# Local attention in a six-stage kernel: values for shifted keys computed, or put together by transfers

## The chip, the cores and the metric

The kernel runs on one core of one Trainium2 chip, as one program with one launch. The time is device time in microseconds (us), the median of three runs. The engines are PE (TensorE; PEld are its weight loads), DVE (VectorE), ACT (ScalarE), POOL (GpSimd) and SP (SyncE, which issues most transfers). All data are 32-bit floats except masks and a few small operands in bf16.

## The reference

Eight sequences of 256 tokens, 128 channels, pass through four layers of different kinds: a gated linear recurrence followed by local attention with a feed-forward block (twice), a Mamba block with a mixture of experts, multi-head attention with a feed-forward block and a second mixture of experts, and a last attention with a ternary linear layer. Only the local attention matters here; it has 8 heads of 64 channels and a window of 64:

```python
bk, bv = (look_around(bk), look_around(bv))   # keys of the window before and of the own window
sim = jnp.einsum('bhwid,bhwjd->bhwij', bq, bk)
mask = (i < j) | (i > j + WINDOW) | (j == -1)
sim = jnp.where(mask, -jnp.finfo(sim.dtype).max, sim)
attn = jax.nn.softmax(sim, axis=-1)
out = jnp.einsum('bhwij,bhwjd->bhwid', attn, bv)
```

So each window of 64 queries sees 128 keys: its own window and the one before. Of a sequence of 256 tokens, window 0 and 1 need keys 0 to 127, window 2 needs keys 64 to 191, window 3 keys 128 to 255. The order of the keys within such a set doesn't matter to the result, as long as scores, mask and values have the same order.

## The kernel before

**Stages.** The program has six stages: `rglru` (the recurrence), `local_mamba` (local attention with its feed-forward block, twice, then Mamba, for each sequence), `moe1`, `chunked` (multi-head attention), `moe2`, `typed` (the last layer). In the profile `local_mamba` runs from about 46 us to 790 us; `chunked` begins at about 860, `moe2` at 1270, `typed` at 1440.

**`local_mamba`.** `one_sequence` runs two local blocks (`local_block`, l = 0 and 1) for a sequence; `mamba_sequence` then takes its result. `interleave` keeps four sequences of local blocks in flight, beside the second half of the recurrence and the Mamba of the sequences before. There are 8 x 2 = 16 local blocks.

**A local block.** `local_qk` makes four products of 128 tokens x 512 channels (q and k, two token tiles each; tile `qk`), with norms and rotation on ACT, DVE and POOL, and transposes q and k to channels x tokens. `local_attention` then makes the values: three products `vps`, for tokens 0 to 127, 64 to 191 and 128 to 255, each copied by ACT (L1128) to slot 0, 1 or 2 of tile `v`. Both `qk` and `vps` take their PSUM from tag Q, which has two buffers in this stage. Then, for each of two query tiles: a mask product and the score products into `sc`, the maximum on DVE (`nm`, L1147), eight Exps on ACT (`e`, L1153), a reciprocal on DVE (`rc`, L1157), a scaling on POOL (L1158), eight transposes (`pt`, L981) with copies to `ptsb`, and the output products `o`, which read `v` as the operand that is held. `parts` tells which queries use which keys and which slot:

```python
parts = (((0, P, 0, 0),), ((128, 64, 64, 1), (192, 64, 128, 2)))   # first query, queries, first key, slot of v
```

The first query tile (queries 0 to 127) uses slot 0; of the second, queries 128 to 191 use slot 1 (keys 64 to 191) and queries 192 to 255 use slot 2. The bf16 mask `band` has one column block of 128 keys for each query tile.

**Mamba.** For each sequence, `mamba_sequence` has eight steps m = 0 to 7. A step needs two transfers on SP (`bc`, L1269, 256 KB each, three buffers), four Exps on ACT (`da`, L1302, three buffers), on DVE the product `hs<-u,bc` (L1304), the scan (L1306) and the product `hs<-hs,bc` (L1307), and on PE two products `y`. The `bc` come from a small table `xs` in DRAM that SP writes first (L1261). A `bc` buffer is free once L1307 of three steps earlier is done.

**What sets the order.** The Python code only records the instructions. `_Order` then plans the order on each engine: a list scheduler that takes, among the instructions that are ready, the one of lowest rank, with durations from `LENGTHS`, per-name shifts of rank from `BIAS` (keyed by engine, tile and stage), and `STAY`, a penalty for leaving a PE tile shape or an ACT function table. The planned order is imposed as the program's order on each engine, so every engine, and SP's queue too, works through a fixed list.

Of the kernel before, what the change touches and what calls it, by code (L numbers as in the profile page):

```python
# [23 lines left out]
P = 128  # L24
# [57 lines left out]
def _tables():  # L82
    f = np.float32
    cols, n = [], 0
# [9 lines left out]
    half = np.arange(0, 64, 2, dtype=f)  # L94
# [47 lines left out]
    def mask(bad):  # L142
        return np.where(bad, f(NEG), f(0))
# [3 lines left out]
    w = i % 64  # L147
    madd("band", np.concatenate([mask((i < k0) | (i > k0 + 64)), mask((k0 < w) | (k0 > w + 64))], 1))
# [163 lines left out]
class _Order:  # L312
# [14 lines left out]
    STAY = dict(PE=80, ACT=740)  # L327
    BIAS = {
        "ACT  1": 100, "ACT  5": 585, "ACT bt 3": 5, "ACT bt 5": -775, "ACT d 2": -425, "ACT da 2": -45, "ACT e 2": -5, "ACT e 4": 965, "ACT e 6": -20,
        "ACT got 3": 575, "ACT h 2": -200, "ACT ix 4": 15, "ACT k 2": 265, "ACT lavp 2": 210, "ACT lnrs 1": -10, "ACT lnrs 2": -160, "ACT lnsq 1": -135,  # L330
        "ACT lnsq 2": 15, "ACT ot 2": 10, "ACT ptsb 2": -595, "ACT ptsb 6": -515, "ACT q 2": 20, "ACT qsq 2": 10, "ACT r 2": -5, "ACT rg 1": 10,
        "ACT rg 2": -915, "ACT rn 2": 15, "ACT rs 4": 340, "ACT rs 6": -690, "ACT s 6": 200, "ACT sakq 2": -10, "ACT sg 3": -550, "ACT sh 5": -2525,
        "ACT spe 1": -220, "ACT spt 1": -50, "ACT st 6": 100, "ACT sz 2": 280, "ACT v 2": 885, "ACT vs 4": 320, "ACT xchunked 2": 15, "ACT xs 2": -610,
        "DVE biasfull 3": -335, "DVE biaspart 3": -20, "DVE bt 5": -5, "DVE c 1": 590, "DVE centre 0": 320, "DVE d 2": 10, "DVE decaypart 4": -600,
        "DVE e 4": 570, "DVE four 4": 100, "DVE fs 4": -70, "DVE gate 4": 340, "DVE get 2": 200, "DVE got 4": 530, "DVE identb 0": -50, "DVE k 6": 500,
        "DVE lg 2": 2240, "DVE lo 4": -265, "DVE mv 4": -660, "DVE mv 5": 100, "DVE mv 6": -485, "DVE nm 2": -3975, "DVE nm 6": 4960, "DVE nth 4": -45,
        "DVE oh 2": -725, "DVE oh 5": -10, "DVE ptsb 2": -3895, "DVE ptsb 6": 895, "DVE put 4": -395, "DVE put 5": 55, "DVE q 5": -825, "DVE q 6": -475,
        "DVE rc 2": -1225, "DVE rc 6": 10, "DVE route 2": -55, "DVE s 5": 10, "DVE sares 2": 70, "DVE sel 2": -1590, "DVE sg 3": -140, "DVE sm 4": 2720,
        "DVE spl 1": -215, "DVE ss 2": 370, "DVE st 4": 85, "DVE st 6": 1645, "DVE sum 4": 170, "DVE t 2": 440, "DVE u 2": 250, "DVE vs 4": 50,
        "DVE we 4": 1425, "DVE xc 2": 460, "DVE xla 4": -15, "DVE xlocal 2": -5, "DVE xmoe 5": -200, "DVE xmoe 6": -580, "DVE xpf 4": -370,  # L340
        "DVE xrglru 2": 120, "DVE xsa 4": 80, "DVE z 4": -1990, "PE a 2": -100, "PE acc 5": 155, "PE b 2": -35, "PE bt 3": 75, "PE bt 5": 50,
        "PE cum 2": -995, "PE cum 4": -25, "PE cum 5": -615, "PE fold 2": 2915, "PE g 2": -4155, "PE gate 2": 785, "PE kps 4": 135, "PE less 2": 295,
        "PE lg 2": 1680, "PE lg 4": 50, "PE ln 2": -10, "PE o 2": 10, "PE o 6": -10, "PE pg 5": 150, "PE ps 4": -15, "PE pt 4": -130, "PE pu 3": 220,
        "PE py 3": -200, "PE py 5": 170, "PE qk 2": 25, "PE qkt 2": -720, "PE raw 2": -8675, "PE rows 2": 400, "PE sc 2": -50, "PE sc 4": 65, "PE sc 6": 5,
        "PE v 5": 290, "PE vps 2": 4075, "PE vps 4": 25, "PE wo 2": 75, "PE wo 6": -85, "PE wout 2": -115, "PE xin 2": 1180, "PE xps 2": -2540, "PE y 2": 20,
        "PE z 2": -450, "PE zt 5": 560, "PE zt 6": 25, "POOL d 2": 130, "POOL e 6": -30, "POOL got 4": -200, "POOL h 2": 370, "POOL k 5": 400,
        "POOL k 6": 850, "POOL km 6": 1240, "POOL mean 0": 1510, "POOL places 5": -200, "POOL q 6": 20, "POOL rest 4": -65, "POOL rg 1": -800,
        "POOL rg 2": -200, "POOL rot 2": -400, "POOL s 6": -750, "POOL t 2": 550, "POOL zero 0": -655, "POOL zeros 1": 385, "SP bc 2": -970, "SP cst 3": 5,
        "SP got 3": 355, "SP got 5": 350, "SP rottable 0": 80, "SP rows 4": 210, "SP rowschunked 4": -105, "SP vec 0": -830, "SP w 0": 15, "SP w 3": 115,
        "SP wattn 2": 585, "SP wffn 2": 705, "SP wlocal 0": 1175, "SP wmoe 4": 520, "SP xs 2": -105, "SP ybuf 5": -200,  # L350
    }
    LENGTHS = {
        "ACT  LoadActFuncSet  ": (1178, 1283), "ACT d Ln 128x512 128x512": (535, 640), "ACT da Exp 128x255 128x255": (398, 503),
        "ACT e Abs 128x256 128x256": (460, 565), "ACT e Exp 128x128 128x128": (420, 525), "ACT e Exp 128x256 128x256": (461, 566),
        "ACT e Exp 128x512 128x512": (527, 632), "ACT four Exp 128x2 128x2": (100, 205), "ACT got DMACopy 128x512 128x512": (454, 3611),
        "ACT h TensorCopy 64x255 64x255": (295, 400), "ACT lnrs Exp 128x256 128x256": (315, 420), "ACT ot TensorCopy 128x512 128x512": (486, 591),
        "ACT qsq Square 128x512 128x512": (494, 599), "ACT r Relu 128x256 128x256": (460, 565), "ACT rg Exp 128x1020 128x1020": (1039, 1144),
        "ACT rg Exp 128x1024 128x1024": (998, 1103), "ACT rg Ln 128x1024 128x1024": (950, 1055), "ACT rn Exp 128x16 128x16": (110, 215),
        "ACT rn Ln 128x16 128x16": (112, 217), "ACT rs Exp 128x2 128x2": (96, 201), "ACT rs Ln 128x2 128x2": (98, 203),
        "ACT sh Silu 128x512 128x512": (492, 597), "ACT v TensorCopy 128x512 128x512": (485, 590), "ACT xc Identity 128x256 128x256": (460, 565),  # L360
        "ACT xc Silu 128x512 128x512": (526, 631), "ACT xchunked TensorCopy 128x256 128x256": (263, 368), "ACT xmoe Identity 128x256 128x256": (404, 509),
        "ACT xs TensorCopy 33x256 33x256": (257, 362), "ACT xsq Square 128x128 128x128": (297, 402), "DVE biaspart TensorCopy 96x256 96x256": (197, 282),
        "DVE decay TensorScalarPtr 128x512 128x512": (508, 593), "DVE decaypart TensorCopy 128x512 128x512": (331, 416),
        "DVE four TensorScalarPtr 128x4 128x4": (76, 160), "DVE ge TensorScalarPtr 128x256 128x256": (380, 465),
        "DVE ge TensorScalarPtr 85x256 85x256": (372, 457), "DVE got TensorScalarPtr 128x128 128x128": (258, 343),
        "DVE h TensorTensor 128x256 128x256": (312, 397), "DVE hs TensorScalarPtr 128x1024 128x1024": (2189, 2274),
        "DVE hs TensorTensor 128x1024 128x1024": (1116, 1201), "DVE mv BNStatsAggregate 128x2 128x6": (82, 167),
        "DVE nm TensorTensor 128x8 128x8": (66, 151), "DVE ptsb TensorCopy 128x512 128x512": (589, 674), "DVE rc Reciprocal 128x16 128x16": (160, 245),
        "DVE rc Reciprocal 128x4 128x4": (84, 169), "DVE rc Reciprocal 128x8 128x8": (106, 191), "DVE rg TensorScalarPtr 128x256 128x256": (577, 662),
        "DVE rg TensorTensor 128x1024 128x1024": (1109, 1194), "DVE rottable TensorScalarPtr 128x256 128x256": (261, 346),  # L370
        "DVE s TensorScalarPtr 128x128 128x128": (247, 332), "DVE s TensorTensor 128x256 128x256": (323, 408),
        "DVE sm TensorReduce 128x16 128x512": (593, 678), "DVE ss TensorReduce 128x8 128x512": (594, 679), "DVE st BNStats 128x6 128x128": (197, 282),
        "DVE sum TensorReduce 128x32 128x448": (810, 895), "DVE t TensorScalarPtr 128x256 128x256": (384, 469),
        "DVE t TensorTensor 128x512 128x512": (593, 678), "DVE vec TensorTensor 128x1 128x1": (59, 144), "DVE vec TensorTensor 85x1 85x1": (59, 144),
        "DVE vs TensorCopy 128x512 128x512": (594, 679), "DVE wlocal TensorScalarPtr 128x682 128x682": (481, 566),
        "DVE x TensorScalarPtr 128x256 128x256": (368, 453), "DVE xc TensorScalarPtr 128x254 128x254": (383, 468),
        "DVE xc TensorScalarPtr 128x255 128x255": (384, 469), "DVE xla TensorScalarPtr 128x256 128x256": (442, 527),
# [394 lines left out]
class _Kernel:  # L772
# [346 lines left out]
    def local_attention(self, l, h, w, rot, work, local, small, pools):  # L1119
# [5 lines left out]
        for a in range(3):  # L1125
            ps = self.psum("Q", "vps")
            self.mm(ps, h[:, 64 * a : 64 * a + P], w[:, l, 1024:1536])
            nc.scalar.copy(v[:, a, :], ps)  # L1128
# [1282 lines left out]
```

## Time and profile before

| what | value |
|---|---|
| timed runs | 1627.46, 1628.3, 1633.44 us; median 1628.3 |
| profiled execution | 1644.68 us, span 1642.9 us |
| mean granted TensorE clock | 0.942 |
| busy share of the span | PE 86%, PEld 55%, DVE 67%, ACT 59%, POOL 36% |
| transfers | 77.97 MB, mean 47 GB/s |
| opening of local attention, 46 to 245 us | PE 166.8 of 199 us busy, ACT 153.2, DVE 121.7 |
| local attention beside Mamba, 245 to 690 us | DVE 388.7 of 445 us busy, PE 380.1, ACT 349.8 |

How to read the profile's lines: a group line names the source line, engine and operation, the tile written and the tiles read, the shapes and the number of instructions, then busy us and mean ns of one, then the idle time of the engine just before them and what ended it. A line of waits says who waited for whom, the total in us, how many times, and the longest. A float product is recorded on PE as two matmuls, so counts of records are twice the counts of products. L870 is the helper through which all matmuls are recorded (L868 in the changed kernel); the tile names tell them apart. The profiled execution is 16.4 us longer than the median of the timed runs.

### The profile page before, as it was taken

What the parts mean: (1) busy time and instruction counts of PE and PEld (TensorE: products, weight loads), DVE (VectorE), ACT (ScalarE), POOL (GpSimd) and SP (SyncE); (2) the same over time, 40 slices, a digit from 0 to 9 for tenths busy, and PEclk for the clock granted to TensorE, in tenths of its full rate; (3) what the DMA queues carried; (4) which work ended last, traced back from release to release, by engine and by line L of the source; (5) the groups of instructions that cost most, each with busy time, mean ns of one, the idle gap of its engine ahead of it and who ended that gap; (6) DMA issues with size and microseconds to landing.
All of it is one profiled execution on the core that took longest, in us unless ns stands there. A gap on an engine that the chain in (4) does not pass through costs nothing. (4 is left out here: it accounts for less than half of the span.)

```text
span 1642.9 us, 28581 instructions
## 1 busy us (share of the span) xinstructions
PE 1417.4 (86%) x10826; PEld 909.4 (55%) x10826; DVE 1102.3 (67%) x2182; ACT 968.6 (59%) x2656; POOL 587.5 (36%) x535
## 2 busy tenths in 40 slices
PE   2688998989898887777579999999998899899997
PEld 1354554545554544334366766777675576556664
DVE  5745568898989898698545557554546333279886
ACT  3777888787978869446125545455453222167775
POOL 1334544535462523101431222212212102467774
PEclk7789999989999999779789999999998899999998
DMA  5000012121212223155430000000000130000000
GB/s 199 1 1 1 1 40 65 40 60 45 65 40 65 53 52 91 52 179 189 151 119 1 8 12 11 10 5 8 32 18 24 46 121 26 26 9 8 5 8 11
DMA packets 45113, 77.97 MB, mean 47 GB/s; under 512 B 5580, under 2 KB 21988, under 8 KB 43824
## 3 DMA queue, kind: packets, MB, share of 16 engines
q1 hardware_dynamic: 39648, 70.02, 14.0%
q0 software_dynamic: 3216, 5.07, 1.1%
q8 instruction: 85, 1.39, 0.4%
q10 hardware_dynamic: 2112, 1.05, 0.2%
q14 instruction: 52, 0.43, 0.1%
HBM read 66.87 MB, written 10.76 MB: 47 GB/s over the span
## 5 line engine op out<-in xcount | busy, mean ns | idle before, releaser
L870 PE MATMUL y<-hs,ident 128*128 128x512 f32 x256 | 139.7, 659 | 35.9 <-DVE hs L1307 35.6
L1158 POOL TENSOR_TENSOR e<-e,rc 128x1024 f32<-128x1024 f32 x32 | 78.0, 2437 | 202.7 <-DVE rc L1157 194.3
L1306 DVE TENSOR_TENSOR_SCAN hs<-da,hs 128x1024 f32<-128x1024 f32 x64 | 149.1, 2331 | 0.2
L2259 ACT ACTIVATE e<-sc,nm 128x128 f32<-128x128 f32 (+1 forms) x256 | 105.2, 427 | 46.6 <-DVE nm L2254 40.3
L1153 ACT ACTIVATE e<-sc,nm,rn 128x128 f32<-128x128 f32 x256 | 114.3, 466 | 13.8 <-DVE nm L1148 13.5
L981 PE MATMUL pt<-ident,e 128*128 128x128 f32 x768 | 114.2, 278 | 9.4 <-POOL e L1158 4.9
L1302 ACT ACTIVATE da<-d,na 128x255 f32<-128x255 f32 x256 | 109.3, 504 | 17.5 <-DVE hs L1306 13.7
L1836 POOL TENSOR_TENSOR e<-e,rc 128x512 f32<-128x512 f32 x32 | 34.0, 1064 | 219.8 <-DVE rc L1835 154.2
L981 PEld LDWEIGHTS pt<-ident,e 128*128 128x128 f32 x768 | 88.5, 141 | 42.5 <-issue 16.1
L2262 POOL TENSOR_TENSOR e<-e,rc 128x1024 f32<-128x1024 f32 x48 | 90.8, 1896 | 39.1 <-DVE rc L2261 32.1
L1105 POOL TENSOR_TENSOR t<-t,t 128x512 f32<-128x512 f32 x64 | 83.9, 1316 | 58.0 <-DVE t L1092 51.6
L1811 ACT COPY kp<-kps 128x512 f32<-128x512 f32 x128 | 74.7, 583 | 49.0 <-PE kps L870 46.4
L1658 POOL DMA_INDIRECT got<-ybuf,get x48 | 45.7, 952 | 159.2 <-DMA ybuf<-ys 97.1
L870 PEld LDWEIGHTS y<-hs,ident 128*128 128x128 f32 x256 | 48.5, 205 | 82.5 <-DVE hs L1307 54.2
L1304 DVE TENSOR_TENSOR hs<-u,bc 128x1024 f32<-128x1024 f32 x64 | 84.3, 1328 | 2.9 <-POOL u L1291 2.9
L1307 DVE TENSOR_TENSOR hs<-hs,bc 128x1024 f32<-128x1024 f32 x64 | 80.6, 1260 | 0.0
L1847 ACT COPY vs<-vps 128x512 f32<-128x512 f32 x64 | 37.4, 585 | 67.1 <-PE vps L870 53.6
L983 DVE COPY ptsb<-pt 128x512 f32<-128x512 f32 x104 | 68.8, 675 | 11.6 <-PE pt L981 9.3
L870 PE MATMUL qk<-w_local,h 128*128 128x512 f32 x128 | 69.3, 631 | 7.5 <-DVE t L1092 7.1
L870 PE MATMUL vps<-sa_vp,x_lf 128*32 128x512 f32 x512 | 68.4, 594 | 0.0
L1847 DVE COPY vs<-vps 128x512 f32<-128x512 f32 x64 | 43.3, 682 | 37.2 <-PE vps L870 25.1
L2057 DVE TENSOR_TENSOR sh<-sh,pu 128x512 f32<-128x512 f32 x32 | 22.0, 688 | 67.1 <-PE pu L870 54.0
(380 smaller groups left out, 3782.4 us busy)
## 6 DMA issues: line engine op xcount, KB each, us to landing
bc<-xs SPq DMA_DIRECT2D x128, 256.0 KB
w_moe<-in_e_dram SPq DMA_DIRECT2D x16, 768.0 KB
w_attn<-in_w_dram SPq DMA_DIRECT2D x4, 1024.0 KB
w_local<-in_w_dram SPq DMA_DIRECT2D x2, 1557.0 KB
places<-zeros SPq DMA_DIRECT2D x2, 1280.0 KB
got<-places SPq DMA_DIRECT2D x6, 256.0 KB
ybuf<-ys SPq DMA_DIRECT2D x8, 160.0 KB
x_in<-in_x_dram SPq DMA_DIRECT2D x1, 1024.0 KB
```

Of the source, the lines that this page charges most:

```text
L870: return self.nc.tensor.matmul(out, lhsT, rhs, start=start, stop=stop)
L981: self.last = self.nc.tensor.transpose(pt[:, j * P : (j + 1) * P], src[:, j * P : (j + 1) * P], self.ident)
L1105: nc.gpsimd.tensor_add(t1, t1, t2)
L1153: nc.scalar.activation(e[:, j, g, :], scs[:, j, g, :], AF.Exp, bias=nm[:, j, g : g + 1], scale=rq[:, j, g : g + 1], accum_out=sm[:, j, g : ...
L1158: nc.gpsimd.tensor_tensor(e, e, rc.unsqueeze(3).to_broadcast([P, 2, 4, P]), ALU.mult)
L1302: nc.scalar.activation(da[:, n, c, 1:S], d[:, c, 1:S], AF.Exp, scale=na[:, i : i + 1])
L1304: nc.vector.tensor_tensor(hs, u.unsqueeze(1).to_broadcast(shp), bn, ALU.mult)
L1306: nc.vector.tensor_tensor_scan(line(hs), line(da), line(hs), 0.0, ALU.mult, ALU.add)
L1307: nc.vector.tensor_tensor(hs, hs, cn, ALU.mult)
L1847: i = copy(v[:, c, :, :].rearrange("p a b -> p (a b)"), ps)
L2259: nc.scalar.activation(e[:, i, :], sc[:, i, :], AF.Exp, bias=nm[:, i : i + 1], accum_out=sm[:, i : i + 1])
L2262: nc.gpsimd.tensor_tensor(e, e, rc.unsqueeze(2).to_broadcast([P, n, keys]), ALU.mult)
```

## The change

The values of a sequence are made by two products, for tokens 0 to 127 and 128 to 255, copied by ACT to slots 0 and 2. Slot 1 is put together by two transfers on SP of 64 partitions x 512 floats: partitions 64 to 127 of slot 0 (keys 64 to 127) and partitions 0 to 63 of slot 2 (keys 128 to 191) go to the same partitions of slot 1. Slot 1 thus holds keys 128 to 191 first and keys 64 to 127 second. The score products of queries 128 to 191 read their keys in that order (two runs of 64, swapped), and the first 64 rows of the mask's second block are rolled by 64 columns.

The planner's numbers are changed as a whole: nearly all of `BIAS`, the values of `LENGTHS` (with a new entry for the transfer), and `STAY`. They hold for all stages, so the order changes in all of them. Lines up to the change move up by two, lines behind it down by three (L1269 becomes L1272, L1128 becomes L1127).

```diff
     w = i % 64
-    madd("band", np.concatenate([mask((i < k0) | (i > k0 + 64)), mask((k0 < w) | (k0 > w + 64))], 1))
+    late = mask((k0 < w) | (k0 > w + 64))
+    late[:64] = np.roll(late[:64], 64, 1)
+    madd("band", np.concatenate([mask((i < k0) | (i > k0 + 64)), late], 1))
...
-    STAY = dict(PE=80, ACT=740)
+    STAY = dict(PE=360, ACT=640)
     BIAS = {
...
         v = pools.tile([P, 3, 512], F32, tag="v", name="v")
-        for a in range(3):
+        for t in range(2):
             ps = self.psum("Q", "vps")
-            self.mm(ps, h[:, 64 * a : 64 * a + P], w[:, l, 1024:1536])
-            nc.scalar.copy(v[:, a, :], ps)
+            self.mm(ps, h[:, t * P : (t + 1) * P], w[:, l, 1024:1536])
+            half = slice(64 - 64 * t, P - 64 * t)
+            nc.scalar.copy(v[:, 2 * t, :], ps)
+            nc.sync.dma_start(v[half, 1, :], v[half, 2 * t, :])
...
-                        self.mm(scs[q0 - t * P : q0 - t * P + n, j, g, :], q[r, g, q0 : q0 + n], k[r, g, k0 : k0 + P], False, g == 3)
+                        keys = k[r, g, k0 : k0 + P]
+                        if k0 == 64:
+                            keys = keys.rearrange("p (a b) -> p a b", a=2)[:, ::-1, :]
+                        self.mm(scs[q0 - t * P : q0 - t * P + n, j, g, :], q[r, g, q0 : q0 + n], keys, False, g == 3)
```

## The prediction

> **What bounds the kernel now.** The profiled execution took 1644.68 us with a span of 1642.9; the median of the three timed runs is 1628.3, 16.4 us (1.0%) less. All sums are made against the profiled execution, and their difference is then taken off the median. A difference within 0.5% (8 us) is about what a measurement of this kernel can't tell from no change.
>
> I first cut the span at the stages' seams. Columns are stretch, its length, busy us (and instructions) of PE, PEld, DVE, ACT and POOL, granted clock, DMA share, GB/s.
>
> ```profile
> 0.00:46.00 46.00, 14.66 (x50) 9.18 (x51) 23.53 (x37) 20.66 (x33) 7.70 (x27) 0.78 0.50 178
> 46.00:245.00 199.00, 166.82 (x1083) 99.88 (x1082) 121.73 (x206) 153.24 (x410) 85.48 (x94) 0.92 0.03 9
> 245.00:690.00 445.00, 380.14 (x2122) 223.96 (x2120) 388.73 (x472) 349.84 (x906) 190.80 (x156) 0.96 0.22 57
> 690.00:860.00 170.00, 115.75 (x614) 77.14 (x616) 117.53 (x178) 69.99 (x150) 41.58 (x37) 0.83 0.47 155
> ```
>
> The changed lines run in rows two and three. In the opening (46 to 245: local blocks only, no scan yet) PE is the fullest at 84%, ACT has 77%, DVE 61%. In the middle (245 to 690: local blocks beside the Mamba scans) DVE leads with 87%, PE has 85%, ACT 79%. Later stages (PE 397 of 410 us in the attention stage from 860) hold none of the changed code.
>
> Next the value products alone, in the same two stretches, and the groups of both lines over the first 680 us:
>
> ```profile
> 46.00:245.00 199.00, 19.99 (x36) 6.71 (x36) 0.00 (x0) 10.54 (x18) 0.92 0.03 9
> 245.00:690.00 445.00, 32.42 (x60) 10.62 (x60) 0.00 (x0) 17.45 (x30) 0.96 0.22 57
> ```
> ```profile
> L870 PE MATMUL vps<-w_local,h 128*128 128x512 f32 x96 | 52.4, 642 | 6.7 <-ACT v L1128 5.8 <-DVE t L1092 0.9
> L1128 ACT COPY v<-vps 128x512 f32<-128x512 f32 x48 | 28.0, 594 | 12.9 <-PE vps L870 12.7
> ```
>
> 48 products are 96 records, two each: 52.4 / 48 = 1.09 us of PE for a product, 0.59 us of ACT for its copy. The timeline shows one costly place: three value products share two Q buffers, so the third of the first block stands until ACT, behind two table loads, copies the first out.
>
> ```profile
> 58.43 2.66 PE L870 MATMUL vps<-w_local,h 128*128 128x512 f32 x4
> 65.39 2.07 PE L870 MATMUL vps<-w_local,h 128*128 128x512 f32 x2 [4.29 <-ACT v L1128]
> ```
>
> **Removed, opening.** 18 of the products lie here, so 6 go: 19.99 / 3 = 6.7 us of PE, 10.54 / 3 = 3.5 us of ACT. PE is busy 84% of this stretch, so 6.7 x 0.84 = 5.6 us of it is path. The 4.29 us stand loses its third product, but the next user of the Q buffers, a query product of the second sequence, then waits for the same copy; the built order of the changed kernel puts that copy ahead of the second table load instead of behind it. I credit half, 2.1, ends 0 and 4.3. Opening: -7.7 us, ends 0 and -11.0.
>
> **Removed, middle.** 10 products go: 32.42 / 3 = 10.8 us of PE, 17.45 / 3 = 5.8 us of ACT. DVE sets the pace; it is idle 445 - 388.7 = 56 us, 13%, and PE or ACT time is worth something only there: (10.8 + 5.8) x 0.13 = 2.2. DVE's named waits for the local blocks agree that little is to be had:
>
> ```profile
> DVE ss L1086 <- ACT qsq L1085: 5.2, 9, 1.3
> DVE nm L1147 <- PE sc L870: 5.0, 6, 2.3
> ```
>
> I take -2.2; the ends are 0 and -10.8, all of PE's time.
>
> **Added transfers.** 32 transfers of 64 x 512 floats (128 KB), 4.2 MB in some 600 us: 7 GB/s beside the 57 shown, at a DMA share of 0.22. No row has this transfer. The nearest below is xs, 33 KB: issued at 235.44, and its reader is issued at 236.90, so at most 1.5 us. The nearest above is a 256 KB bc of sequence 1, issued at 341.9 and used at 346.4: at most 4.5 us. What hides it: the first product that reads the middle slot comes late. In the first block the copies of v end at 68.1 and the second query tile's output products start at 101.0; in the built order at least 31 us of PE work stands between a block's value products and that reader, in every block. So 0 at either end; without that cover it would be up to 4.5 us for each of 16 blocks.
>
> "SBUF — State Buffer", section "The DMA setup-cost knee", speaks against the edit: a transfer costs about 2 us whatever its size, 64 partitions move hardly more per second than 32, and an estimate from its fit for 128 KB is 2 + 0.3 = 2.3 us. No row here times a 64-partition transfer; by the page's price the sum is the same.
>
> **Added waits.** The built order gives PE 31 more waits for a DMA, but only 18 more separate wait instructions; DVE's queue shows such instructions at 21 ns, so 0.4 us, taken as 0. SP issues in order. The v transfers of the first six blocks stand before any bc. Later ones stand between bc pairs and wait for ACT's copy, and a bc pair behind them waits too. This is the rival below; for the forecast I take 0, because bc pairs are issued up to three steps ahead of their use.
>
> **Reversed keys.** 128 products (256 records) read their 128 keys as two runs of 64 in swapped order. No PE row shows that. On DVE, L1092 reads such swapped halves at 680 ns where L1090 reads straight at 682. I take 0; the upper end is the step between the two sc forms, 300 against 285 ns: 256 x 15 ns = 4 us. A gain is excluded, since as many columns pass. The changed mask is data only.
>
> **Moved.** The planner's numbers change for every stage, so all five orders move. Counted in the built orders, much stays: 69 table loads in both; before the first scan's products PE has 706 instructions after 715, ACT as many local-block steps; DVE's work ahead of each sequence's scans agrees within 3 us; PE's changes of tile shape fall from 508 to 492. Behind 690 us nothing is removed, and PE is idle 97 us of 953 there; a tenth of that, 10 us either way, is my estimate of what new orders may move. I take 0.
>
> **Sum.** -7.7 - 2.2 = -9.9: 1644.7 becomes 1634.8, and the median 1628.3 becomes 1618.4, faster by 0.6%.
>
> **PE's fullness, weighed.** The sum turns on row two, PE 84%. "Trainium Kernel Development and Optimization", section "Best Practices", says that matmul busy time does not tell how close TensorE is to its limit and LDWEIGHTS busy share does. The row has 99.88 of 199 us of LDWEIGHTS, 50%. If that weight replaced 0.84, the opening would give 6.7 x 0.5 + 2.1 = 5.5 us instead of 7.7, and the total would be 7.7: just inside no change.
>
> **Rivals.** (1) Latency, not PE, sets the opening: each block is a chain through five engines, and POOL waits 52.7 us for DVE's rc there, ACT 8.6 for query products. For it: four sequences in flight leave PE idle 16%. Against: in that stretch DVE's longest wait is for PE's scores (15.8 us). Then only the 2.1 and 2.2 are gained, -4: 1624, no change. The new orders giving back what the blocks gain (-10 + 10) ends there too: 1628.
>
> (2) The bc queue, slower. In the built order the bc pair of step 3 in sequences 0, 1 and 2, and of step 5 in sequence 3, stands behind a v transfer whose copy ACT makes after that step's four da Exps. Today those bc leave when the buffer is freed (421.9 in sequence 2) while da ends at 427.6 and the step starts at 429.4. Behind the copy: 427.6 + 0.6 + two issues of 0.4 + 4.5 = 433.5, 4.1 us late; the same working gives 2.1, 0 and 2.9 for the others, 9 us on DVE, the fullest engine. If ACT also puts a group of eight e Exps (168.5 us / 256 x 8 = 5.3 us) ahead of each copy, 21 more: up to 30. With 21 the net is +11: 1639. It decides from 2.5 us late per place (4 x 2.5 = the 9.9 gained). Against it: DVE has other work in its queue between steps, and the landing is an upper bound.
>
> (3) The change does what it says: PE has 16 products fewer, ACT 16 copies fewer, SP 32 transfers more in the built order, so a no-op is ruled out.
>
> **Numbers.** Forecast (gain over 8 us) 0.50; rival 1 and cancelled orders 0.26; rival 2 with worse orders 0.24. Low end: 6.7 + 4.3 + 10.8 = 21.8 all gained plus 4 from orders: 1602. High end: rival 2 at its net +11, with 1 of the possible 4 us for reversed keys: 1640. Outside 0.1 is left on each side. The forecast's own range is 1606 to 1620.
>
> **What would show it.** vps at 64 records and about 35 us, v copies at 32 and about 19; the first scan some 8 us earlier than 252.7; the stand at 65.39 gone or halved; no wait of o for a DMA; the scan's first product (hs<-u,bc) never waiting for bc. Wrong if the first scan starts no earlier, if DVE waits for bc in sequences 0 to 3, or if the stretch behind the last scan grows.

## The result and the profile after

| kernel | median (runs) | lowest to highest |
|---|---|---|
| before | 1629.12 us (4) | 1627.46 to 1633.44 |
| after | 1642.56 us (4) | 1642.09 to 1646.42 |

The changed kernel is slower: 1.0081 of the time before, 95% interval 1.0061 to 1.0101. The forecast was 1618.4, its range 1602 to 1640. The profiled execution of after took 1642.59 us, its span is 1640.8, the mean granted clock 0.938.

The same stretches as before, then the value products alone in the first two of them (stretch, its length, busy us and instructions of PE, PEld, DVE, ACT and, in the first fence, POOL, then clock, DMA share, GB/s):

```profile
46.00:245.00 199.00, 160.28 (x1090) 98.56 (x1089) 121.27 (x211) 149.85 (x403) 84.76 (x94) 0.91 0.07 17
245.00:690.00 445.00, 375.77 (x2094) 217.72 (x2092) 392.95 (x469) 343.36 (x894) 189.12 (x154) 0.95 0.26 61
```
```profile
46.00:245.00 199.00, 12.41 (x24) 4.07 (x24) 0.00 (x0) 7.07 (x12) 0.91 0.07 17
245.00:690.00 445.00, 22.66 (x40) 8.06 (x40) 0.00 (x0) 11.36 (x20) 0.95 0.26 61
```

The work that was to go is gone: of the value products 7.6 us in the opening (19.99 - 12.41) and 9.8 us in the middle. The groups of both lines over the first 690 us say the same, and all idle time of PE in front of the value products has vanished (6.7 us before, 0.0 now):

```profile
L868 PE MATMUL vps<-w_local,h 128*128 128x512 f32 x64 | 35.1, 639 | 0.0
L1127 ACT COPY v<-vps 128x512 f32<-128x512 f32 x32 | 18.4, 587 | 3.1 <-PE vps L868 3.0
```

The timeline of PE at the first block: the stand of 4.29 us is down to 0.35 at the query product, since ACT now copies the first values earlier.

```profile
57.50 1.02 PE L868 MATMUL vps<-w_local,h 128*128 128x512 f32 x2
...
60.54 1.02 PE L868 MATMUL vps<-w_local,h 128*128 128x512 f32 x2
61.92 1.12 PE L868 MATMUL qk<-w_local,h 128*128 128x512 f32 x2 [0.35 <-ACT v L1127]
```

The added transfers, from the groups of DMA issues (KB each, median us from issue to landing):

```profile
v<-v SPq DMA_DIRECT2D x32, 128.0 KB, 2.2
```

The longest of the landings seen took 6.4 us. No product `o` waits for a DMA, and DVE's waits between 245 and 690 us have no row for `bc`. DVE's waits for the local blocks, though, have grown; the rows that answer to those shown of before:

```profile
DVE ss L1084 <- ACT qsq L1083: 9.9, 14, 2.4
DVE nm L1150 <- PE sc L868: 6.0, 7, 2.4
```

So all that was removed is off the engines, and still the first scan starts at 254.7 us (before: 252.7).

**Stage by stage.** The stages are cut where a first or last instruction marks them: the first query product, the first scan, the last scan, the first product of the attention stage (`kps`), its last value product, the first product of the last stage (`proj`), the end of ACT's last copy; the span is some 5 us longer than the sum of a row, since it takes in the transfer of the result. Lengths in us, one profiled execution each, kernels as named in the experiments; the upper part is from three chips on which the unchanged kernel takes about 1628 to 1630 us, the lower from one on which it takes 1645.8:

| kernel | first query product at | opening | scans | first experts | attention | second experts | last stage | span |
|---|---|---|---|---|---|---|---|---|
| before again (e1) | 45.7 | 207.3 | 534.7 | 61.8 | 390.2 | 144.9 | 238.7 | 1628.0 |
| after again (e2) | 43.1 | 211.9 | 536.8 | 64.0 | 388.7 | 151.6 | 243.6 | 1644.3 |
| edit, old order (k1) | 46.4 | 208.8 | 527.7 | 61.8 | 389.7 | 145.5 | 238.7 | 1623.2 |
| edit, new order of opening (k5) | 46.0 | 211.6 | 528.3 | 62.0 | 387.9 | 146.8 | 238.7 | 1625.8 |
| edit, new order early (k3) | 44.9 | 210.4 | 537.5 | 62.9 | 387.8 | 147.1 | 239.0 | 1634.2 |
| edit, new order of attention (i1) | 46.7 | 207.9 | 531.5 | 62.2 | 388.5 | 145.7 | 238.8 | 1625.9 |
| edit, copies first (j2) | 45.0 | 210.7 | 527.4 | 62.0 | 389.8 | 145.5 | 238.7 | 1623.7 |
| before, new order late (h2) | 44.8 | 207.3 | 534.8 | 61.9 | 390.5 | 150.3 | 243.2 | 1637.5 |
| before, middle product twice (j1) | 44.6 | 209.5 | 533.3 | 62.3 | 389.3 | 144.9 | 238.6 | 1627.2 |
| edit, old order (f1) | 44.4 | 207.8 | 531.3 | 62.4 | 396.0 | 144.7 | 247.5 | 1638.5 |
| removal only (f2) | 45.9 | 207.7 | 531.6 | 62.3 | 396.1 | 144.9 | 247.2 | 1640.3 |
| addition only (f3) | 47.1 | 207.4 | 534.8 | 61.9 | 396.9 | 144.9 | 247.2 | 1644.7 |
| after, old order late (h1) | 45.3 | 210.5 | 535.7 | 65.1 | 397.9 | 145.6 | 247.5 | 1652.6 |

Between e1 and e2, on one chip, the loss of 16.3 us of span is made of +4.6 in the opening (which begins 2.6 us earlier), +2.1 in the scans, +2.2 in the first experts, -1.5 in the attention stage, +6.7 in the second experts and +4.9 in the last stage. The last two hold none of the edit. Executions of one and the same program differ as well: f1 and k1 by 3.6 us in the scans, after (387.3 us) and e2 by 1.4 in the attention stage. A difference of that size in one row shows little by itself.

### The profile page after: what moved, and what is told of

Its sections match the earlier page's. It is cut to its first block, busy times and chain, and to the rows that moved or that the text cites. A ratio compares the mean times of both kernels' runs of the same rounds, so it can differ in the third digit from the quotient of the medians.

```text
span 1640.8 us, 28593 instructions
## 1 busy us (share of the span) xinstructions
PE 1410.0 (86%) x10794; PEld 897.5 (55%) x10794; DVE 1110.1 (68%) x2182; ACT 960.8 (59%) x2640; POOL 582.3 (35%) x535
## 3 DMA queue, kind: packets, MB, share of 16 engines
q10 hardware_dynamic: 2112, 1.05, 0.2%
## 4 chain that ended last, share of the span: by engine, by line
PE 55%; DVE 20%; ACT 14%; issue 6%; POOL 3%; DMA 2%; SPq 0%; DVEq 0%; POOLq 0%; ACTq 0%
PE vps L868 8%; PE kps L868 7%; PE sc L868 6%; PE out L868 4%; PE pu L868 4%; ACT e L1156 3%; PE pt L979 3%; PE pg L868 3%; DVE hs L1309 3%; DVE hs L1310 2%; PE y L868 2%; ACT da L1305 2%; DVE hs L1307 2%; PE o L868 2%; PE hps L868 2%
## 5 line engine op out<-in xcount | busy, mean ns | idle before, releaser
L868 PE MATMUL y<-hs,ident 128*128 128x512 f32 x256 | 144.4, 679 | 29.8 <-DVE hs L1310 29.6
L1161 POOL TENSOR_TENSOR e<-e,rc 128x1024 f32<-128x1024 f32 x32 | 70.7, 2208 | 211.8 <-DVE rc L1160 211.5
L1839 POOL TENSOR_TENSOR e<-e,rc 128x512 f32<-128x512 f32 x32 | 33.5, 1048 | 205.2 <-DVE rc L1838 117.9
L2265 POOL TENSOR_TENSOR e<-e,rc 128x1024 f32<-128x1024 f32 x48 | 90.9, 1899 | 42.7 <-DVE rc L2264 27.0
L1661 POOL DMA_INDIRECT got<-ybuf,get x48 | 45.7, 952 | 153.3 <-DMA ybuf<-ys 101.1
L1307 DVE TENSOR_TENSOR hs<-u,bc 128x1024 f32<-128x1024 f32 x64 | 89.7, 1418 | 1.0 <-POOL u L1294 0.9
L868 PE MATMUL sc<-msk,identb 128*128 128x512 bf16 (+2 forms) x224 | 48.2, 356 | 21.5 <-ACT e L1156 21.2
```

The source lines that it names most:

```text
L868: return self.nc.tensor.matmul(out, lhsT, rhs, start=start, stop=stop)
L1161: nc.gpsimd.tensor_tensor(e, e, rc.unsqueeze(3).to_broadcast([P, 2, 4, P]), ALU.mult)
L1307: nc.vector.tensor_tensor(hs, u.unsqueeze(1).to_broadcast(shp), bn, ALU.mult)
L2265: nc.gpsimd.tensor_tensor(e, e, rc.unsqueeze(2).to_broadcast([P, n, keys]), ALU.mult)
```

## The experiments

A ratio below is not the quotient of the two medians beside it: it is formed from all the runs, with its 95% interval.

**Both kernels again.** No edit, as the base for the rest.

> The kernel before, unchanged, once more, for a second profiled execution and for the spread of its times. Its profile was 16 us longer than its timed runs; the changed kernel's profiled execution (1642.6 us) was not longer than its timed ones. If that one profile of before was merely an unlucky execution: times 1626 to 1634 us, ratio 1.000 within 0.003, and this profile's span is near 1628 us, with the missing 14 us to be found in named stages. If profiling itself lengthens this kernel: the profile is near 1643 us again.

Measured: 1628.39 us, 0.9997 of before (0.9982 to 1.0013). The profiled execution took 1629.83 us, so profiling by itself doesn't lengthen this kernel.

> The changed kernel, unchanged, on the chip of the next two. All theories: 1640 to 1646 us, ratio 1.006 to 1.010 to the kernel before.

Measured: 1645.51 us, 1.0100 (1.0072 to 1.0128). The loss stands on another chip.

**Code and planner's numbers, crossed.** The new code with the old `BIAS`, `LENGTHS` and `STAY`; and the old code with the new ones.

```diff
-    STAY = dict(PE=360, ACT=640)
+    STAY = dict(PE=80, ACT=740)
     BIAS = {
...
```

> The two products, the two transfers, the reversed keys and mask, but planned with the old numbers (BIAS, LENGTHS, STAY of before; only the new transfer's entry added). Theory A (the new planner numbers cost the time, the edit itself gains): 1618 to 1624 us, 5 to 10 us faster than before. Theory B (the edit costs by itself: transfers, their waits or the reversed reading): 1636 to 1645 us. Theory C (any order not planned with its own fitted numbers costs): 1632 to 1645 us, with the loss in stages that hold none of the edit.

Measured: 1634.63 us, 1.0039 (1.0023 to 1.0054).

```diff
-    STAY = dict(PE=80, ACT=740)
+    STAY = dict(PE=360, ACT=640)
     BIAS = {
...
```

> Three products, no transfers, keys and mask in the old order, but planned with the new numbers (BIAS, LENGTHS, STAY of after). Theory A: slower than after, 1645 to 1655 us, since it has the new numbers' loss and lacks the edit's gain. Theory B: as before, 1626 to 1634 us. Theory C: 1640 to 1655 us, with the loss outside the local blocks too.

Measured: 1663.87 us, 1.0220 (1.0191 to 1.0249); its scans take 549.9 us. That is above what any of the three theories had. Each crossing plans a third and a fourth order, so neither separates the edit from the order. What they show is the size of an order's worth: with the old code, the new numbers cost 33.5 us against the old ones. The next runs therefore take the order out of the planner's hands.

**The edit in the old order.** The planner is replaced by a written-down list, before's order on all five engines, with the third products and copies struck out and the transfers put on SP behind their copies. All kernels from here on have such a list, and only the lists and the few lines shown differ.

```diff
     def impose(self):
-        order, _ = self.plan()
+        flat, order, at = np.frombuffer(zlib.decompress(base64.b64decode(FIXED)), np.int32), {}, 0
+        for e in ("ACT", "DVE", "PE", "POOL", "SP"):
+            n = int(flat[at])
+            order[e] = flat[at + 1 : at + 1 + n].tolist()
+            at += n + 1
```

> The whole edit (two products, two transfers, reversed keys and mask), with the planner taken out: every engine keeps the order of the kernel before, written down as a list; the third products and copies are struck from it, and each transfer stands on SP where its copy was due. If the forecast's working was right and only the new orders spoiled it: 8 to 12 us faster than before (ratio 0.993 to 0.995). If the removed PE and ACT time was never on the path: within 2 us of before. If the edit itself costs (transfers, waits, reversed reading): 3 to 6 us slower, as with the new plan from old numbers.

Measured: 1641.91 us on a chip where before takes 1645.81: 0.9977 (0.9963 to 0.9991). The edit by itself is a gain of 3.9 us, between the first two cases that were expected. By the profiles it lies in the scans (531.3 against 534.8 in f3 on the same chip); the opening gains nothing.

**Removal alone, addition alone.** f2 strikes the third products and copies and lets the middle queries read slot 0; f3 keeps three products and adds transfers, mask and swapped keys.

```diff
-        for a in range(3):
+        for t in range(2):
             ps = self.psum("Q", "vps")
-            self.mm(ps, h[:, 64 * a : 64 * a + P], w[:, l, 1024:1536])
-            nc.scalar.copy(v[:, a, :], ps)
+            self.mm(ps, h[:, t * P : (t + 1) * P], w[:, l, 1024:1536])
+            nc.scalar.copy(v[:, 2 * t, :], ps)
...
-        parts = (((0, P, 0, 0),), ((128, 64, 64, 1), (192, 64, 128, 2)))
+        parts = (((0, P, 0, 0),), ((128, 64, 64, 0), (192, 64, 128, 2)))
```

> The old order as a list, third products and copies struck, and nothing put in their place: queries 128 to 191 read slot 0 for their values, keys and mask as before, no transfers. It leaves out the values of keys 64 to 191. If the removed time is worth something: 8 to 12 us faster than before, and f1 minus this is the cost of the transfers. If it is off the path: within 2 us of before.

Measured: 1641.59 us, 0.9979 (0.9965 to 0.9993), the same as the whole edit.

```diff
         for a in range(3):
             ps = self.psum("Q", "vps")
             self.mm(ps, h[:, 64 * a : 64 * a + P], w[:, l, 1024:1536])
             nc.scalar.copy(v[:, a, :], ps)
+        for t in range(2):
+            half = slice(64 - 64 * t, P - 64 * t)
+            nc.sync.dma_start(v[half, 1, :], v[half, 2 * t, :])
... (mask and keys as in the changed kernel)
```

> The old order as a list, all three products and copies kept, and the two transfers, the reversed keys and the mask added; the transfers overwrite slot 1. If transfers and their waits are hidden and the reversed reading is free: within 2 us of before. If they cost: 5 to 15 us slower, and f1 lies between this and f2.

Measured: 1644.55 us, 0.9997 (0.9984 to 1.0011). Transfers, their waits, SP's longer queue, swapped keys and changed mask together cost nothing that can be measured. (In f1 and k1, not in f3, one weight load of `o` waits 0.8 us for a transfer.)

**The changed kernel with before's order in the last two stages**, the converse of what comes next.

```diff
- order of the instructions of moe2 and typed: after's
+ order of the instructions of moe2 and typed: before's
```

> The changed kernel with its own order up to the attention stage, but the instructions of the last two stages (moe2 and typed) placed among themselves as in the kernel before. These stages hold none of the edit. If the new order of the late stages costs 11 of the 15 us, as the stretches of the two profiles say (moe2 +6, typed +5): 1632 to 1637 us, some 11 faster than the changed kernel. If those stretches are longer only because they start from another state: 1640 to 1646 us.

Measured: 1653.15 us, 1.0051 (1.0033 to 1.0070). The two stages are back at 145.6 and 247.5 us, before's lengths on that chip (144.9 and 247.2). What is left, +7.3 us, lies mostly ahead of them: 6.5 of the 7.9 us by the spans against f3. The changed kernel itself has no run on this chip, so the 11 us that were expected can't be read off directly.

**Before with the new order in the last two stages.** Nothing but the order of instructions that the edit doesn't touch.

```diff
- order of the instructions of moe2 and typed: before's
+ order of the instructions of moe2 and typed: after's
```

> The code of before in before's written-down order, with one thing changed: the instructions of the last two stages (second experts, typed), which hold none of the edit, stand among themselves as in the changed kernel. Theory (new orders cost time where nothing was edited): the second experts grow from 144.9 to about 151 us and the last stage is some 5 us longer than in before on the same chip where that chip is a fast one; 8 to 12 us in all, ratio 1.005 to 1.007, everything ahead of 1270 us within 1 us of before. Rival (those stages suffer from what comes before them in the changed kernel): no change, ratio 0.999 to 1.001.

Measured: 1636.46 us against 1628.15, 1.0045 (1.0030 to 1.0060). By the spans, +5.4 us in the second experts and +4.6 in the last stage against j1, which ran on the same chip in the old order. The trace shows how. First PE's row for the same 20 us of the second experts, j1 (old order) and then h2 (new order), columns as above:

```profile
1279.00:1299.00 20.00, 20.00 (x105) 13.80 (x103) 6.80 (x11) 5.46 (x10) 0.00 (x0) 1.00 0.25 61
```
```profile
1279.00:1299.00 20.00, 19.25 (x80) 11.93 (x81) 3.85 (x6) 3.73 (x7) 0.00 (x0) 0.85 0.37 94
```

80 matmul records in place of 105 at a granted clock of 0.85 in place of 1.00. The timeline of PE there, again j1 and then h2 (start us, us, what, idle before and releaser):

```profile
1277.07 1.12 PE L1035 MATMUL pg<-x_chunked,w_shared 128*128 128x512 f32 x2 [1.82 <-ACT sh L2218]
1278.03 1.02 PE L1035 MATMUL pu<-x_chunked,w_shared 128*128 128x512 f32 x2
1278.89 1.05 PE L1035 MATMUL acc<-w_shared,sh 128*128 128x128 f32 x8
...
1281.50 1.04 PE L1816 MATMUL bt<-ident,got 128*128 128x128 f32 x8
```
```profile
1277.26 1.38 PE L1036 MATMUL pg<-x_chunked,w_shared 128*128 128x512 f32 x2 [1.92 <-ACT sh L2218]
1279.75 0.45 PE L1816 MATMUL bt<-ident,got 128*128 128x128 f32 x1 [1.11 <-DMA got<-places]
1279.99 1.92 PE L1036 MATMUL acc<-w_shared,sh 128*128 128x128 f32 x8
1281.70 1.91 PE L1036 MATMUL pu<-x_chunked,w_shared 128*128 128x512 f32 x2
1283.41 1.74 PE L1036 MATMUL pg<-x_chunked,w_shared 128*128 128x512 f32 x2
```

The old order fills PE with products of the shared expert until the gathered rows (`got`) have landed. The new order puts the first transposition of those rows (`bt`) right behind the next product, and PE stands 1.11 us for the transfer. The clock falls as well: three groups take 1.92, 1.91 and 1.74 us in place of about 1.05, 1.02 and 1.02. That is 1.1 + 2.5 = 3.6 of the 5.4 us. In after the same wait is there with 0.92 us, in e2 with 1.6.

The wait for the transfer did not make the clock fall. In h2 the granted clock rose at 1274.59 us and fell at 1278.01, while the wait begins at 1278.64; in after, too, the fall comes ahead of the wait, and in e2 the two come together. Two rows of h2, then the row of j1 that answers to the first (the DMA share is summed over the packets that begin in a stretch, so it can exceed 1):

```profile
1274.60:1278.00 3.40, 1.48 (x4) 0.30 (x2) 0.69 (x1) 0.60 (x1) 1.96 (x2) 1.00 0.24 67
1278.02:1284.82 6.80, 5.69 (x14) 3.22 (x14) 0.69 (x1) 0.60 (x1) 0.00 (x0) 0.50 1.13 295
```
```profile
1274.62:1278.02 3.40, 1.57 (x8) 0.91 (x7) 0.69 (x1) 0.60 (x1) 1.96 (x2) 1.00 0.33 86
```

In these 3.4 us PE stood 1.92 us in h2 and 1.82 in j1, both times for ACT's `sh`; PE was busy 1.48 us and 1.57 us, and then the clock fell in h2 and stayed in j1. All three executions with the new order of this stage (h2, after, e2) lose the clock here, and it stays down for 6.8 us. Of the twelve with before's order nine keep it; in k3 and k5 it is back after 3.4 us, in h1 after 6.8. Why it fell, and whether the wait for the transfer then kept it down longer, was not tried.

In the last stage PE's waits for DVE's copies of the transposed attention weights grow, again j1 and then h2 (who waited for whom, us in total, times, longest):

```profile
PE o L1035 <- DVE ptsb L1148: 1.1, 4, 0.3
```
```profile
PE o L1036 <- DVE ptsb L1149: 4.8, 13, 0.6
```

These 3.7 us are most of the 4.6. That they are the cause, and not only beside it, was not tried.

**The middle value product twice.** The reverse of the removal, for PE alone.

```diff
-            self.mm(ps, h[:, 64 * a : 64 * a + P], w[:, l, 1024:1536])
+            for _ in range(1 + (a == 1)):
+                self.mm(ps, h[:, 64 * a : 64 * a + P], w[:, l, 1024:1536])
             nc.scalar.copy(v[:, a, :], ps)
```

> The code and order of before with the middle value product of every block computed twice into the same PSUM buffer: 16 products (17.5 us of PE) more, no copy, no transfer, no further buffer. The exact reverse of the PE work that the edit removes. Theory (in the opening PE work is not on the path, since the chain through ACT, DVE and POOL sets it; beside the scans it counts a little): first scan within 1 us of before, the stretch of the scans 2 to 4 us longer, ratio 1.001 to 1.003. Rival (PE's 84% busy share says what its work is worth, and the removal lost its gain to something else): first scan 5 to 6 us later, 7 to 10 us in all, ratio 1.004 to 1.006.

Measured: 1628.92 us against 1628.15, 0.9998 (0.9986 to 1.0009). The value products take 24.45 us in the opening (19.89 in e1) and 39.72 in the middle (32.42): 11.9 us of PE more by the records, at no cost in the total. It is not PE's work alone that changed, though: the mean granted clock of the timed runs is 0.946, of before on that chip 0.942. The first scan comes 2.2 us later, counted from the first query product; the scans take it back (533.3 against 534.7). Nearer to the theory than to its rival, though the theory's small loss beside the scans isn't seen either.

**ACT's copies ahead of the table loads.** The edit in the old order, with the first copy of the first block ahead of the recurrence's Exp and the second right behind it.

```diff
 ACT, first block:
+    copy v<-vps (slot 0)
     Exp rg (with its table load)
+    copy v<-vps (slot 2)
     table load, Exp rg, Exp rn
-    copy v<-vps (slot 0)
     Exp rn
-    copy v<-vps (slot 2)
```

> The whole edit in before's written-down order, and in the first block ACT makes the two copies of the values before and right after the Exp of the recurrence that holds them up, ahead of the table loads that stand there. The 4.3 us stand of PE for the Q buffer should go. Theory (DVE's 6.55 us reciprocal of the recurrence stands ahead of the first maximum, so the first block's scores wait for DVE in any case): the stand is gone, the maximum starts no earlier than the end of that reciprocal, and the first scan is within 1 us of the edit in the old order; the ratio stays 0.997 to 0.998. Rival (the prediction's term: half of the stand is path): first scan 2 us or more earlier, ratio 0.996 or less.

Measured: 1626.80 us against 1628.15, 0.9994 (0.9983 to 1.0005). In the edit in the old order the stand had not gone, it had moved to the next user of the Q buffers; this is k1's timeline of PE, where 4.05 us stand ahead of a query product:

```profile
67.35 2.08 PE L1033 MATMUL qk<-w_local,h 128*128 128x512 f32 x2 [4.05 <-ACT v L1292]
```

In j2 that product starts at 60.76, right behind the values, but PE then stands 5.89 us for POOL:

```profile
67.75 1.12 PE L1273 MATMUL qkt<-ident,t 128*128 128x128 f32 x4 [5.89 <-POOL t L1270]
```

The first scores start 26.4 us after the first query product in j2 as in k1 (71.36 and 72.76 us). And even these wait for DVE:

```profile
68.28 6.55 DVE L1198 RECIPROCAL rg<-rg 128x1024 f32<-128x1024 f32 x1
74.75 1.16 DVE L1315 TENSOR_REDUCE nm<-sc 128x8 f32<-128x1024 f32 x1
```

The score products end at 73.4 us, but the maximum over them waits in DVE's queue behind a reciprocal of 6.55 us that belongs to the recurrence. In j2 that chain starts later still (the reciprocal 23.3 us after the first query product, 21.7 in k1 and 20.8 in f1), as ACT now makes a copy ahead of the Exp that feeds it, and the first scan comes 2 us later than in k1 and 3 us later than in f1. The expectation had that within 1 us; the sign of it speaks for the chain through ACT, DVE and POOL and against PE. The scans are as long as k1's (527.4 against 527.7 us); the totals of the two kernels are not told apart.

**The edit with the new order of the attention stage only.** The one stage that was shorter in after.

```diff
- order of the instructions of chunked: before's
+ order of the instructions of chunked: after's
```

> The whole edit in before's written-down order, with the instructions of the attention stage alone (860 to 1270 us) standing among themselves as in the changed kernel, the one stage that was shorter there (387.3 to 388.7 us against 390.2). Theory (a stage's length belongs to its own order): that stage 1.5 to 3 us shorter than with the old order on the same chip, a ratio of 0.996 to 0.9975, the best of all. Rival (it was shorter because its start was put elsewhere by the stages around it): no difference from the edit in the old order, 0.9977, or up to 2 us more.

Measured: 1625.81 us against 1628.15, 0.9983 (0.9970 to 0.9996). The stage is 388.5 us long, 389.3 to 390.5 in the other three kernels on that chip: 1 to 2 us. But k3 and k5 below, which have before's order in this stage, take 387.8 and 387.9. In them, as in after, PE's clock stands at half for 2.7 to 2.8 us of the stage, in the other kernels of the table for 5.0 to 6.3. So at least a part of the difference comes with what lies ahead of the stage, as the rival had it, and that the new order itself gives anything is not shown. The total is not told apart from the edit in the old order.

**Where the rest of the loss lies.** Three runs on one chip: the edit in the old order, the same with the new order up to the first experts, and the same with the new order of the opening alone.

```diff
- order of the instructions of rglru, local_mamba, moe1: before's
+ order of the instructions of rglru, local_mamba, moe1: after's
```

> The edit in before's written-down order once more, on the chip of the two runs below, as what they are compared with. Ratio 0.997 to 0.9985, the first scan within 1 us of before's as counted from the first query product, the stretch of the scans 2 to 4 us shorter.

Measured: 1624.60 us against 1627.76, 0.9988 (0.9974 to 1.0003). Against e1 the first scan comes 1.5 us later and the scans are 7.0 us shorter; both lie outside what was expected.

> The edit in before's written-down order, with the instructions of all stages up to the first experts standing among themselves as in the changed kernel, and the attention stage, the second experts and the last stage as in before. Theory (the rest of the loss is the new order of these stages): 7 to 12 us slower than the edit in the old order, ratio 1.002 to 1.005, the opening 3 to 5 us, the scans 3 to 7 us and the first experts 1 to 2 us longer, the stages behind as in before. Rival (the loss ahead of 1270 us comes of how the stages meet): within 3 us of the edit in the old order, ratio 0.997 to 0.9995.

Measured: 1636.58 us, 1.0068 (1.0043 to 1.0093): 12.0 us above k1, at the upper end of what was expected (the ratio is above it). By the profiles 9.8 us lie in the scans (537.5 against 527.7; 6.2 against f1's), 1.6 in the opening. The scans of the second sequence begin 7.1 us later (338.2 in place of 331.1), those of the third only 1.3; then the lag grows again, to 9.5 at the seventh (701.8 in place of 692.3) and 9.9 at the last scan (792.8 in place of 782.9). DVE's largest waits for the local blocks between 245 and 690 us, in k1 and then in k3:

```profile
DVE ss L1249 <- ACT qsq L1248: 5.2, 9, 1.3
...
DVE nm L1315 <- PE sc L1033: 2.1, 3, 1.0
DVE rc L1325 <- ACT e L1321: 1.7, 2, 1.4
```
```profile
DVE ss L1249 <- ACT qsq L1248: 9.7, 14, 2.1
DVE nm L1315 <- PE sc L1033: 6.1, 7, 2.4
DVE rc L1325 <- ACT e L1321: 6.0, 5, 2.1
```

9.0 us have become 21.8: the new order lets DVE, the fullest engine there, wait for the local blocks' own chain more often. Its other waits fell, though, and DVE is as busy in that stretch (393.6 us against 392.5). So these waits by themselves don't account for the lag, and which placement does the harm is not settled.

> The edit in before's written-down order, with the 1403 instructions that both planners put ahead of the first scan standing among themselves as in the changed kernel. Theory (the new order of the opening costs what the opening grew by): the first scan 3 to 5 us later, counted from the first query product, and the total 2 to 5 us above the edit in the old order, ratio 0.9985 to 1.001. Rival (the later first scan is taken up by the scans behind it, as where the middle product was made twice): the total within 1 us of the edit in the old order, 0.997 to 0.9985.

Measured: 1624.66 us, 0.9983 (0.9967 to 1.0000), 0.1 us from k1, though the first scan comes 2.8 us later. By the timed runs, a few us at the first scan don't reach the end, as in j1. The profile doesn't show where they are made good: the profiled execution was the slowest of the twelve (1627.57 us), its scans are no shorter than k1's, and its span is 2.6 us longer.

## Why the prediction was wrong, step by step

- **Removed, opening (-7.7): failed.** At a fixed order the opening is 207.7 to 208.8 us long in f1, f2, i1 and k1 and 207.3 to 207.4 in before: the gain is 0 or a little below. Both terms failed. The first took 6.7 us of products off PE and 84% of that off the time. Here is the opening of f3 and then of f1, on one chip, first whole and then the value products alone:

```profile
47.10:254.50 207.40, 171.75 (x1102) 103.19 (x1102) 128.25 (x218) 160.66 (x428) 93.10 (x99) 0.92 0.06 16
44.40:252.20 207.80, 169.04 (x1090) 102.17 (x1090) 127.99 (x217) 157.65 (x422) 93.07 (x99) 0.90 0.06 16
```
```profile
47.10:254.50 207.40, 21.07 (x38) 7.11 (x38) 0.00 (x0) 11.12 (x19) 0.92 0.06 16
44.40:252.20 207.80, 14.17 (x26) 4.93 (x26) 0.00 (x0) 7.62 (x13) 0.90 0.06 16
```

  6.9 us of value products are gone, but PE is busy only 2.7 us less: the granted clock is 0.90 in place of 0.92, and the other products take 4.2 us longer. What was gained became idle time, 38.8 us in place of 35.7. The second term, half of the stand, was worth nothing either: the stand moved to the next query product, and where that was removed (j2), to POOL, while DVE's reciprocal of 6.55 us held the first maximum all the same. In the changed kernel, where the stand is down to 0.35 us, the maximum goes ahead of the reciprocal (68.50 and 69.63 us), but the small step behind it, which the Exps need, still stands after it:

```profile
76.09 0.10 DVE L1151 TENSOR_TENSOR nm<-nm,rn 128x8 f32<-128x8 f32 x1
76.29 0.46 ACT L1156 ACTIVATE e<-sc,nm,rn 128x128 f32<-128x128 f32 x1 [5.53 <-DVE nm L1151]
```

  So the first Exp comes 32.2 us after the first query product, in before 30.1. This was traced for the first block only; what sets the rest of the opening stays open. PE's work is not free there either: 4.6 us more of products (j1) made the opening 2.2 us longer.
- **Weight of PE.** By the Trainium skill's page "Trainium Kernel Development and Optimization", section "Best Practices", the prediction had as its other weight PE's LDWEIGHTS share of 50%, which would have given 5.5 us for the opening. The runs give 0: in this stretch neither share was the price.
- **Removed, middle (-2.2): near.** At a fixed order the scans are 3.2 to 7.3 us shorter (f1, f2, i1, k1, j2 against 534.7 to 534.8), and of it 1.4 to 4.2 us are left in the totals. DVE's share of idle time came near as a weight. That it is the reason was not tried, nor whether PE's products or ACT's copies brought the gain.
- **Added transfers (0): right.** f3 costs nothing and f1 equals f2. They land in 2.2 us by the median, between the bounds of 1.5 and 4.5; the longest, 6.4 us, is above them, and nobody waits for it. The estimate of 2.3 us from the Trainium skill's page "SBUF — State Buffer", section "The DMA setup-cost knee", agrees with that row; its rule against small transfers is for those that set the time, and these don't.
- **Added waits, reversed keys (0 and 0): right**, both inside f3.
- **Moved (0, either way 10): failed, and decided the result.** The new orders cost 12.0 us up to the first experts (k3 against k1) and 8.3 in the last two stages (h2 against before). With the edit's -3.2 (k1) that makes 17; e2 shows 15.2 against before and the result 13.4, so the pieces add up to within a few us. What was counted in the built orders (table loads, instructions ahead of the first scan, changes of tile shape) did not see the losses, as far as they were found: a transposition put ahead of the landing of its rows, 13 waits for DVE's copies in place of 4. For the stages behind 690 us the end of 10 was wide enough, only the sign was open; for the scans, where the new orders cost 9.8, no price was set at all, because DVE's work ahead of each sequence agreed within 3 us.
- **Rivals.** Rival 1 named both mechanisms that the runs support, a chain through several engines in the opening and orders that give back the gain, but let the second end at no change. Rival 2 was not seen: no wait for `bc` in after, and f3, with the transfers in SP's queue, is no slower. Its side was right, its mechanism was not.
- **What would show it.** The counts came as written, and the first scan, named as the sign of an error, started 2 us later in place of 8 earlier. The stretch behind the last scan, named as another, grew by 12.3 us (e2 against e1).

## What to carry to other kernels

When a change moves the whole order of a planned kernel, price the orders as a change of their own, stage by stage, also where nothing was edited; here they cost some 20 us and the edit gained 3. To know what an edit is worth, hold the order fixed. And before crediting work taken off an engine that is 84% busy, look for the instruction that stands next in the queue of the engine which consumes its result: here, in the first block, a reciprocal of 6.55 us on DVE. And look at the granted clock: work taken off PE can come back as slower products.

The edit in the old order (f1, k1) is faster than both kernels, by 0.1 to 0.2% against before (the interval of f1 leaves no change out, that of k1 just takes it in) and by about 1% against after; no run beat it clearly.

## What the hardware showed

- **The clock moves in steps of 3.41 us.** In every trace here each stretch at full or half clock is a whole number of 3.41 us long, but for the last, which the end cuts off. In h2 the clock fell after a step in which PE was busy 1.48 of 3.40 us, in e2 after 1.61 us, in j1 it held after 1.57; so the border lies near half and these rows don't fix it. In the Trainium skill, "TensorE: Matmul & The Clock Gate", section "What's actually happening", lets the clock fall after an idle window of about 3.4 us and rise after as long a busy one. The rise came here after a step that was all busy; the fall came without an idle step, in h2 with no single stand of more than 1.92 us.
- **Less work on PE, a slower clock.** The mean granted clock of the timed runs is 0.936 in f1 and f2, which have fewer products, and 0.940 in f3 and in before on that chip; in j1, with more products, it is 0.946 against 0.942. So a part of what was taken off PE came back in the products that were left (4.2 us in f1's opening).
- **The same program on two chips.** Before takes 1645.81 us on one chip and 1627.76 to 1630.32 on three others. The runs on the slower one (f1, f2, f3, h1) have a longer attention stage and last stage and little else. The prediction's profile is of that kind: against e1 its stages up to the first experts agree within 0.4 us, but the attention stage takes 396.9 us in place of 390.2 and the last stage 247.2 in place of 238.7, though the granted clock is 0.94 in both. That is where 15.2 of its 16.4 us above the median came from. So a stage's length is compared on one chip.
